# Own steps of a 7x7 depthwise convolution: eleven dealt stores, and bands and a first tile asked for by GpSimd

## The chip, the core and the metric

The kernel runs on one core of one Trainium2 chip. The metric is the device time of one execution in microseconds (us); a time is the median of several runs. Traces and pages come from one profiled execution, whose own time stands beside its span.

## The reference

The input x is (8, 96, 96, 192) in f32. Two layers follow each other; everything is f32.

```python
x1  = x  + L0(gn(x))      # gn: group norm, 32 groups
out = x1 + L1(gn(x1))

def L0(v):                # 192 -> 384 -> 192 channels
    local = conv3x3_depthwise(v @ W_in + b_in)
    mixed = 0.25 * (four directional EMA scans of local) + local
    return (layernorm(mixed) * ln_g + ln_b) @ W_out + b_out

def L1(v):                # 192 -> 768 -> 192 channels
    y = conv7x7_depthwise(v) + dw_bias
    y = gelu((layernorm(y) * ln_gamma + ln_beta) @ w0 + b0)
    return (y @ w1 + b1) * gamma
```

The group norm takes its sums over a whole image, so the 7x7 convolution of one half of the batch can begin when x1 of that half is complete.

## The kernel before

The order of the instructions on each engine is written out by hand: inside `tc.manual_schedule()` every engine gets its instructions in the order in which the program names them. A DMA is issued by an engine's queue (SyncE's is `SPq` in the trace, ScalarE's `ACTq`, GpSimd's `POOLq`), and a wait at the head of such a queue holds all that is behind it. Tiles come from pools; a tile whose place in memory was used before waits for the last user of that place.

The work runs in five stages. Times in brackets are those of the profiled execution, counted from the start of the span.

- Stage A: group norm of x and the projection W_in.
- Stage B: the 3x3 convolution, the four scans, their mixing.
- Stage C (to about 2633 us): layer norm, W_out and the residual. It makes x1 in tiles `x1c` (line 1097), 12 tiles in all, from a pool `c_x` of two buffers. Each tile is written to the DRAM array `X1` by `store_c` (line 1133) in 12 stores of 384 KB, in runs of 768 bytes. One store goes out with each unit of work (`stores.pop(0)()`); those of the last tile are left over at the end of the loop and are issued on SyncE in one go (`for store in stores: store()`).
- Stage D, the "own" steps (2630 to about 2960 us): steps n = 0 to 18 of the 7x7 convolution, with `NI` = 16 and `N1` = 19. Step n has a channel group of 12 channels and half of the batch. It needs six loads of x1 (`load_raw`, line 887, 384 KB each, tiles `raw`, three pairs numbered t), the convolution's weights written as a band matrix (`load_band`, line 897, 624 KB, tile `band`; `spread`, line 925, copies it to the other 64 partitions), the group norm applied to the raws (`scale_steps`, lines 919 and 921, tile `xin`), the matmuls (`conv_d`, line 1244, 144 a step in the trace), 12 evictions by ScalarE that add the bias (line 1254, tile `yo`), and stores of the result to the DRAM array `Y` (`store_d`, lines 1271, 1275, 1276: two of 810 KB and four of 27 KB, on SyncE). Raws are asked for two steps ahead by GpSimd, bands two steps ahead by SyncE. `yo` has two buffers, so step n's evictions wait for the stores of step n-2.
- Stage E (2960 us to the end): the last pass over 144 tiles of Y, `y_n`. `load_y` (lines 1305 and 1311, tiles `ya` and `yb`, 40 loads each: 32 of them of 60 KB, in runs of 384 bytes) fetches a tile; `norm_steps_e` gives the chain of its layer norm (sums, line 1388; `total`, 1354 to 1362; centering, 1381; square, on ScalarE; powers, 1415, on GpSimd); lines 1451 and 1461 are the matmuls with w0, 1481 those with w1, 1492 the residual, 1500 the output. The other steps of the convolution (19 to 31) are spliced into it.

The first tiles of the last pass are loaded while the own steps still run. `main_y` names 24 loads of y_0, which go out between the channels of own steps 12, 13 and 14, two after each `conv_d(n, c)`, on ScalarE's queue. `rest_y` holds the tile's memory set-up (n = 11), the other 16 loads of y_0 (n = 16, after the convolution) and the 40 loads of y_1 (n = 17), the last two on SyncE. In own step 17 the layer norm's chain for y_0 begins (`chain`), and in step 18 that for y_1 (`nxt`). The scalings of xin for step 18 are `steps[:per_t]` on VectorE (those of t = 0) and `on_scalar` on ScalarE (t = 1, 2).

The order of one own step, in the loop over n, is: raws of n + 2, band of n + 2, stores of n - 1, then the scalings for n + 1, then the convolution of n, then `on_scalar` and `rest_y`.

Of the kernel before, what the change touches and what calls it, by code (L numbers as in the profile page):

```python
# [8 lines left out]
F32 = mybir.dt.float32  # L9
# [92 lines left out]
def conv_blocks_kernel(  # L102
# [31 lines left out]
    nc = tc.nc  # L134
    B, S, _, D = x.shape
# [10 lines left out]
    by_tile = dict(reuse_waits="tile")  # L146
# [18 lines left out]
    WQ = WV // NV  # L165
# [85 lines left out]
    with ExitStack() as ph:  # L251
        cp = ph.enter_context(tc.tile_pool(name="a_const", bufs=1, **by_tile))
        xp = ph.enter_context(tc.tile_pool(name="a_x", bufs=6, **by_tile))
# [259 lines left out]
        with tc.manual_schedule():  # L513
# [71 lines left out]
    NI = len(place)  # L585
# [212 lines left out]
    NI = D // GC  # L798
# [92 lines left out]
    def load_band(n, eng=None):  # L891

        i = todo[n][1]
        pool = early if n >= N1 else (early, gp, d_pools[1])[n % 3]
        bands[n] = band = pool.tile([128, GC, ZW], F32, tag="band", name="band1")
        g = i % 2
        (eng or nc.sync).dma_start(
            band[g * 64 : (g + 1) * 64].rearrange("q c l -> q (c l)"),
            Z2_d[:, i * GC : (i + 1) * GC].rearrange("r c l -> r (c l)"),
        )  # L900
# [104 lines left out]

    with ExitStack() as ph:
        cp = ph.enter_context(tc.tile_pool(name="c_const", bufs=1, **by_tile))
        xp = ph.enter_context(tc.tile_pool(name="c_x", bufs=2, **by_tile))
        ip = ph.enter_context(tc.tile_pool(name="c_in", bufs=4, **by_tile))
        sp = ph.enter_context(tc.tile_pool(name="c_small", bufs=2, **by_tile))  # L1010
        ps_s = ph.enter_context(tc.tile_pool(name="c_ps_s", bufs=1, space=PSUM, **by_tile))
# [3 lines left out]
        NJ3 = 3  # L1015
# [9 lines left out]
                pick[:, b], ident[:, b * QH : b * QH + 1].to_broadcast([128, 128])  # L1025
            )
        nc.vector.memset(mean_w, 1.0 / C)
        lnb = xp.tile([128, NJ3, D, WQ], F32, tag="x1c", name="lnb")
        lnb = lnb.rearrange("p j c v -> p (j c v)")[:, : NC * 128]
        lnb = lnb.rearrange("p (m k) -> p m k", m=NC)  # L1030
        ps = ps_s.tile([128, 512], F32, tag="gn_ps", name="ps_w")
# [109 lines left out]
        steps, stores, first_d = [], [], []  # L1141
        with tc.manual_schedule():
            weights = load_weights()
            for u in range(n_u + 1):
                if weights and u >= 8:
                    with nc.allow_non_contiguous_dma(reason="one value per partition"):
                        nc.scalar.dma_start(*weights.pop(0))
                if u + 3 < n_u:
                    ahead.append(load_c(u + 3))
                if stores:  # L1150
                    stores.pop(0)()
                if u == n_u - 36:
                    early_d = [lambda: load_band(0)]
                    early_d += [lambda t=t: load_raw(0, t) for t in range(NT)]
                    early_d += [lambda: load_band(1)]
                if u >= n_u - 36 and u % 3 == 0 and early_d:
                    early_d.pop(0)()
                if u == n_u - 14:
                    first_d += scale_steps(0)
                    for t in range(NT):  # L1160
                        first_d.insert((t + 1) * 9 - 1, lambda t=t: load_raw(1, t))
                if u >= n_u - 14:
                    for step in first_d[:3]:
                        step()
                    del first_d[:3]
                if held is not None:
                    rs = scale_c(held[1])
                if u < n_u:
                    mt, xr = ahead.pop(0)
                    nc.gpsimd.tensor_tensor(  # L1170
                        xr, xr, cst.unsqueeze(1).to_broadcast([128, NJ3, D]), ALU.add
                    )
                    var = sp.tile([128, NJ3], F32, tag="var", name="var")
                    pa = ps_o.tile([128, 2, D + 1], F32, tag="po", name="po")
                    pb = ps_o.tile([128, 2, D + 1], F32, tag="po", name="po")
                    pos = [pa[:, 0], pa[:, 1], pb[:, 0]]
                    for j in range(NJ3):
                        block_c(mt, pos[j], var, j)
                if steps:
                    for step in steps.pop(0):  # L1180
                        step()
                if held is not None:
                    n, v = divmod(u - 1, WQ)
                    if v == 0:
                        x1c = xp.tile([128, NJ3, D, WQ], F32, tag="x1c", name="x1c")
                    finish_c(x1c, v, held[0], rs, held[2])
                    if v == WQ - 1:
                        steps += group_steps(x1c, n)
                        stores += [
                            lambda x=x1c, n=n, j=j, q=q: store_c(x, n, j, q)  # L1190
                            for j in range(NJ3)
                            for q in range(NX)
                        ]
                held = (pos, var, xr) if u < n_u else None
            for step in first_d:
                step()
            for store in stores:
                store()
            for step in sum(steps, []):
                step()  # L1200

    WE = 8
    NJ3 = 3
# [58 lines left out]
    def store_d(n):  # L1262

        hf, i = todo[n]
        yf = yos.pop(n).rearrange("q l n c v -> q l (n c v)")
        e = 3 * PH
        m = HG * PH
        for k in range(2):
            part, at = divmod(2 * i + k, YG)
            y_d = Y_d[hf][part][:, at].rearrange("r b a n -> r (b a n)")  # L1270
            nc.sync.dma_start(
                y_d[e : e + NB * m].rearrange("(l q) n -> q l n", q=m),
                yf[k * 64 + e : k * 64 + e + m],
            )
            nc.sync.dma_start(y_d[:e], yf[k * 64 : k * 64 + e, 0])
            nc.sync.dma_start(y_d[ROWS - e :], yf[k * 64 + KB - e : k * 64 + KB, NB - 1])
# [228 lines left out]
    with tc.manual_schedule():  # L1505
        with tc.tile_pool(name="d_own", bufs=1, side="right", **by_tile) as own:
            d_pools[1] = own
            make_xin(1)
            load_band(2)
            make_yo(1)  # L1510
            norms = norm_c(1, bank)
            y_0, y_1 = load_y(0), load_y(1)
            main_y = {
                NI - 4: [y_0[1 + q * 5 + b] for q in (0, 1) for b in range(NH)],
                NI - 3: [y_0[1 + q * 5 + b] for q in (2, 3) for b in range(NH)],
                NI - 2: [y_0[1 + q * 5 + b] for q in (4, 6) for b in range(NH)],
            }
            rest_y = {
                NI - 5: y_0[:1],
                NI: [y_0[1 + q * 5 + b] for q in (5, 7) for b in range(NH)]  # L1520
                + [y_0[1 + q * 5 + NH] for q in range(8)],
                NI + 1: y_1,
            }
            for n in range(N1):
                if n + 2 < N1:
                    for t in range(NT):
                        load_raw(n + 2, t)
                    if n:
                        load_band(n + 2)
                if n:  # L1530
                    store_d(n - 1)
                if n >= 3 and norms:
                    norms.pop(0)()
                if n == 10:
                    make_weights(bank())
                steps = scale_steps(n + 1) if n + 1 < N1 else []
                last, on_scalar = [], []
                if n == NI + 1:
                    chain = norm_steps_e(0)
                    per_t = len(steps) // NT  # L1540
                    on_scalar = steps[per_t:-1]
                    steps = steps[-1:] + chain[:3] + steps[:per_t]
                    on_scalar.insert(per_t, chain[3])
                    chain = chain[4:]
                elif n == NI + 2:
                    nxt = norm_steps_e(1)
                    steps = chain[:2] + nxt[:3] + chain[2:]
                    on_scalar = nxt[3:4]
                    chain = nxt[4:]
                for step in steps:  # L1550
                    step()
                for c in range(GS):
                    conv_d(n, c)
                    for step in main_y.get(n, [])[2 * c : 2 * c + 2]:
                        step(nc.scalar)
                for step in on_scalar + rest_y.get(n, []):
                    step()
            store_d(N1 - 1)
            load_band(N1)
            for t in range(NT - 1):  # L1560
                load_raw(N1, t)
# [8 lines left out]
        for n in range(N1, len(todo)):  # L1570
            more = n + 1 < len(todo)
            scales = scale_steps(n)
            per_t = len(scales) // NT
# [28 lines left out]
        for u in range(n_u + 1):  # L1602
            n, t = divmod(u, per)
# [5 lines left out]
            norm, chain = chain, norm_steps_e(u + 2) if u + 2 < n_u else [lambda: None] * 7  # L1609
# [81 lines left out]
```

## Time and profile before

| | |
|---|---|
| Median of 3 runs | 5508.98 us (5501.92 to 5525.27) |
| Profiled execution | 5497.31 us, of which the span is 5495.5 us |
| Mean granted clock of TensorE | 0.983 |
| TensorE busy | 5277.4 us, 96% of the span, 42206 matmuls |
| VectorE / ScalarE / GpSimd busy | 63% / 47% / 43% of the span |
| DMA traffic | 1015 MB, mean 185 GB/s |

In the profile's groups the own steps' convolution and stage E's convolution steps share line 1244 (4608 matmuls, 420.7 us busy, with 95.7 us idle before them). A row of the timeline reads: start in us, length in us, engine, line of the program, operation, output <- inputs, tile sizes, count, and in square brackets the idle time before it and what ended it. A `q` behind an engine's name is its DMA queue, where a row spans the first issue to the end of the last. A row of the windows gives for one stretch of time each engine's busy time and instruction count, the granted clock, the share of time that the 16 DMA engines were busy, and GB/s.

### The profile page before, as it was taken

To read this page: it belongs to the slowest core of one execution; us is meant where nothing else is said; L and a number is where in the kernel's file an instruction comes from. 1 tells how busy PE (TensorE), PEld (TensorE's weight loads), DVE (VectorE), ACT (ScalarE), POOL (GpSimd) and SP (SyncE) were. 2 spreads that over 40 slices of the span, in tenths; PEclk is the share of its full clock that TensorE was granted. 3 is DMA by queue.
4 is the path that set the end of the run, shared out by engine and by line. 5 is a ranking of instruction groups with operands and counts; after the bars stand their busy time and mean duration, and the time that the engine had idled before them with its cause. 6 is when DMAs were issued, how large, how long until landed. Compare 5 with 4: busy or idle time off the path is not lost. (4 is left out here: it accounts for less than half of the span.)

```text
span 5495.5 us, 108054 instructions
## 1 busy us (share of the span) xinstructions
PE 5277.4 (96%) x42206; PEld 3357.6 (61%) x42206; DVE 3449.8 (63%) x6722; ACT 2586.1 (47%) x5778; POOL 2367.0 (43%) x2060
## 2 busy tenths in 40 slices
PE   6999989999999899999787899999999999999999
PEld 4666643333333799899444566666666676766767
DVE  6556549999999455555555545555566666656654
ACT  2444447777777466565434444444433333333332
POOL 1211128888888555555322232222233333333332
PEclk9999989999999999999888999999999999999999
DMA  7999869999998799899997454555433232333231
GB/s 219 286 289 276 244 188 245 244 244 243 245 243 218 233 291 294 263 287 308 287 302 176 120 137 121 131 138 136 114 89 80 79 79 79 88 90 86 79 79 41
DMA packets 793246, 1015.28 MB, mean 185 GB/s; under 512 B 331151, under 2 KB 668768, under 8 KB 790688
## 3 DMA queue, kind: packets, MB, share of 16 engines
q1 hardware_dynamic: 676488, 633.41, 44.1%
q0 software_dynamic: 84848, 334.59, 18.5%
q10 hardware_dynamic: 31400, 40.37, 3.3%
q8 instruction: 333, 5.46, 0.4%
q14 instruction: 177, 1.45, 0.1%
HBM read 603.70 MB, written 419.95 MB: 186 GB/s over the span
## 5 line engine op out<-in xcount | busy, mean ns | idle before, releaser
L1481 PEld LDWEIGHTS hp<-w1g,g 128*128 128x128 f32 x6912 | 1117.9, 190 | 140.7 <-issue 83.4
L1481 PE MATMUL hp<-w1g,g 128*128 128x192 f32 x6912 | 1174.9, 329 | 0.0
L1470 ACT ACTIVATE g<-hp,b0g 128x512 f32<-128x512 f32 x864 | 519.8, 692 | 1209.4 <-PE hp L1461 1186.1
L1500 POOL DMA_DIRECT2D out_dram<-xo x288 | 211.3, 734 | 1569.5 <-DVE xo L1492 1488.0
L1492 DVE TENSOR_TENSOR xo<-hp,r 128x384 f32<-128x384 f32 x288 | 229.1, 795 | 983.5 <-PE hp L1481 979.2
L1451 PE MATMUL hp<-yT,w0w 128*128 128x512 f32 x1728 | 779.3, 597 | 19.6 <-DVE yT L1436 19.6
L1080 PE MATMUL po<-wc,mt 128*128 128x193 f32 x3456 | 685.5, 334 | 9.8 <-DVE x1c L1097 9.2
L662 PE MATMUL pl<-pin,band 34*32 34x380 f32 (+1 forms) x13824 | 629.4, 490 | 17.5 <-issue 17.5
L746 POOL TENSOR_TENSOR mo<-mo,z 128x768 f32<-128x768 f32 x286 | 598.9, 2094 | 4.5 <-ACT mo L687 0.4
L1080 PEld LDWEIGHTS po<-wc,mt 128*128 128x128 f32 x3456 | 554.9, 191 | 41.3 <-ACT mean L1082 30.8
L1451 PEld LDWEIGHTS hp<-yT,w0w 128*128 128x128 f32 x1728 | 321.3, 190 | 379.7 <-issue 346.0
L695 DVE TENSOR_TENSOR_SCAN z<-decay,loc 128x768 f32<-128x768 f32 x288 | 505.9, 1757 | 38.7 <-ACT loc L671 9.6
L1244 PE MATMUL hp<-xin,band 63*64 63x372 f32 (+1 forms) x4608 | 420.7, 501 | 95.7 <-ACT yo L1254 35.2
L704 DVE TENSOR_TENSOR_SCAN z<-decay,z 128x768 f32<-128x768 f32 x288 | 498.4, 1731 | 0.1
L662 PEld LDWEIGHTS pl<-pin,band 34*32 34x32 f32 x13824 | 236.1, 107 | 392.8 <-issue 385.9
L1415 POOL TENSOR_TENSOR rs<-tot,neg_half 32x32 f32<-32x32 f32 x72 | 394.7, 5481 | 120.3 <-DVE tot L1413 92.5
L683 PE MATMUL pa<-loc,mix 128*32 128x384 f32 x3456 | 431.9, 493 | 0.0
L686 PE MATMUL pa<-last,down 96*32 96x384 f32 x1152 | 426.8, 493 | 0.9 <-ACT mo L687 0.9
L1461 PE MATMUL hp<-yT,w0w 64*128 64x512 f32 x1728 | 419.5, 611 | 0.0
L1254 ACT ACTIVATE yo<-hp,dwb 128x384 f32<-128x384 f32 x384 | 197.0, 584 | 435.6 <-PE hp L1244 285.0
L671 ACT COPY loc<-pl 128x384 f32<-128x384 f32 x576 | 248.0, 483 | 310.7 <-PE pl L662 310.7
L395 PE MATMUL pm<-xT,win 128*128 128x384 f32 x1152 | 392.4, 491 | 0.0
(155 smaller groups left out, 7237.6 us busy)
## 6 DMA issues: line engine op xcount, KB each, us to landing
pin<-P SPq DMA_DIRECT2D x192, 576.0 KB
P<-po POOLq DMA_DIRECT2D x95, 1152.0 KB, 9.9
mt<-M SPq DMA_DIRECT2D x192, 384.0 KB
xq<-in_x_dram SPq DMA_DIRECT2D x96, 576.0 KB
xr<-in_x_dram SPq DMA_DIRECT2D x192, 288.0 KB
X<-x1c SPq DMA_DIRECT2D x144, 384.0 KB
out_dram<-xo POOLq DMA_DIRECT2D x288, 192.0 KB, 2.5
r<-X SPq DMA_DIRECT2D x35, 1536.0 KB
```

The lines of the kernel that those rows point to most:

```text
L662: nc.tensor.matmul(pls[g][at * RB : (at + 1) * RB, :, lo:hi], band[rows, c, kh, :], pin[rows, c, :, NJ - 1 - j, lo + kh - 1 : hi + kh - 1] ...
L683: nc.tensor.matmul(pa[at], mix[:, i, at], loc[:, q], start=True, stop=True)
L686: nc.tensor.matmul(pa[at], down[:, to], last[:, q], start=True, stop=True)
L695: nc.vector.tensor_tensor_scan(zf, decay_f, loc.rearrange("p q n -> p (q n)"), 0.0, ALU.mult, ALU.add)
L704: nc.vector.tensor_tensor_scan(zr, decay_f, zr, 0.0, ALU.mult, ALU.add)
L746: eng.tensor_tensor(m, m, z, ALU.add)
L1080: nc.tensor.matmul(po, lhs[m], wc[:, m], start=(m == 0), stop=(m == NC - 1))
L1244: nc.tensor.matmul(pys[g][k * 64 : (k + 1) * 64, :, lo:hi], band[rows, k * GS + c, d * ZS : d * ZS + 64], xin[rows, :, :, k * GS + c, lo + ...
L1451: nc.tensor.matmul(hps[m, q], w0w[:, 0, m * 128 : (m + 1) * 128], yT[:, 2 * q], start=True, stop=False,)
L1461: nc.tensor.matmul(hps[m, q], w0w[p, 1, m * 128 : (m + 1) * 128], yT[p, 1], start=False, stop=True,)
L1470: nc.scalar.activation(g[:, m, q], hps[m, q], AF.Gelu, bias=b0g[:, m : m + 1], scale=1.0)
L1481: nc.tensor.matmul(po[:, q], g[:, m, q, k * 128 : (k + 1) * 128], w1g[:, m], start=(m == 0), stop=(m == NE - 1),)
```

## The change

Five things change; the arithmetic does not.

1. The pool `c_x` of two buffers becomes two pools of one buffer each, `xps[0]` and `xps[1]`, taken in turn, the last tile x1c from `xps[0]`. So each of the two has its own place in memory, and the pool of the own steps, `d_own`, lies over the other one.
2. The 12 last stores of x1 are not issued at the end of stage C. They are kept in `late_x` and issued on SyncE in the own steps: two in step 0, one each in steps 1 to 10, after the stores of step n - 1.
3. Bands 2 to 18 are issued by GpSimd instead of SyncE (bands 0, 1 and 19 stay).
4. y_0's loads go to GpSimd: the 24 of `main_y` come from ScalarE's queue, the 16 of `rest_y` at n = 16 from SyncE's. Those of y_1 stay on SyncE.
5. In step 17 the eight scalings of t = 0 stand ahead of the first three steps of the layer norm's chain on VectorE, instead of behind them.

```diff
-        xp = ph.enter_context(tc.tile_pool(name="c_x", bufs=2, **by_tile))
+        xps = [
+            ph.enter_context(tc.tile_pool(name=f"c_x{n}", bufs=1, **by_tile)) for n in range(2)
+        ]
...
-                        x1c = xp.tile([128, NJ3, D, WQ], F32, tag="x1c", name="x1c")
+                        x1c = xps[1 - n % 2].tile([128, NJ3, D, WQ], F32, tag="x1c", name="x1c")
...
             for step in first_d:
                 step()
-            for store in stores:
-                store()
+            late_x = stores
             for step in sum(steps, []):
                 step()
...
-            load_band(2)
+            load_band(2, nc.gpsimd)
...
                     if n:
-                        load_band(n + 2)
+                        load_band(n + 2, nc.gpsimd)
                 if n:
                     store_d(n - 1)
+                for step in late_x[: 1 if n else 2]:
+                    step()
+                del late_x[: 1 if n else 2]
...
-                    steps = steps[-1:] + chain[:3] + steps[:per_t]
+                    steps = steps[-1:] + steps[:per_t] + chain[:3]
...
                 for c in range(GS):
                     conv_d(n, c)
                     for step in main_y.get(n, [])[2 * c : 2 * c + 2]:
-                        step(nc.scalar)
-                for step in on_scalar + rest_y.get(n, []):
+                        step(nc.gpsimd)
+                for step in on_scalar:
                     step()
+                for step in rest_y.get(n, []):
+                    if n == NI:
+                        step(nc.gpsimd)
+                    else:
+                        step()
```

More of the change, by code (lines that the diff above doesn't have):

```diff
@@ L1027, in conv_blocks_kernel @@
         nc.vector.memset(mean_w, 1.0 / C)
-        lnb = xp.tile([128, NJ3, D, WQ], F32, tag="x1c", name="lnb")
+        lnb = xps[0].tile([128, NJ3, D, WQ], F32, tag="x1c", name="lnb")
         lnb = lnb.rearrange("p j c v -> p (j c v)")[:, : NC * 128]
```

## The prediction

> **What bounds the kernel now.** I read the page's slices first. A slice is 137.4 us (5495.5 / 40).
>
> ```profile
> PE   6999989999999899999787899999999999999999
> ...
> DMA  7999869999998799899997454555433232333231
> ```
>
> TensorE is full nearly everywhere, save slice 0 and slices 19 to 22 (2610 to 3160 us). There DMA is full at first (9s in slices 19 and 20) and then falls. Every edit lies between 2610 and 2990 us. Second, the chain of work that ended last:
>
> ```profile
> PE 26%; issue 1%; DVE 0%; POOL 0%; ACT 0%; POOLq 0%
> ```
>
> From about 3072 us to the end it is TensorE alone, so a microsecond won before 3072 us arrives whole at the end, and so does one lost. Third, the windows of the stretch (columns: window, us, then busy us of PE, PEld, DVE, ACT, POOL, then granted clock, DMA share, GB/s):
>
> ```profile
> 2632.00:2657.00 25.00, 24.02 (x286) 11.59 (x286) 19.75 (x59) 19.82 (x43) 10.62 (x18) 0.93 1.01 254
> 2657.00:2680.00 23.00, 0.75 (x7) 0.29 (x2) 0.29 (x1) 1.05 (x2) 0.00 (x0) 0.56 1.07 293
> 2680.00:2840.00 160.00, 142.24 (x1572) 81.87 (x1570) 105.23 (x295) 59.94 (x120) 54.19 (x68) 0.93 1.02 319
> 2840.00:2908.00 68.00, 51.68 (x493) 33.88 (x497) 26.89 (x77) 24.09 (x48) 13.35 (x19) 0.84 0.97 254
> ```
>
> The 16 DMA engines are full (share 0.97 to 1.07) for 276 us, while TensorE idles 23 + 16 us in two of the windows. An own step moves 6 raws of 384 KB, a band of 624 KB and stores of 2 x (810 + 27 + 27) KB: 4656 KB, 4.77 MB, 14.9 us at 319 GB/s. Its 144 matmuls take 12.3 us (142.24 / 1572 x 144 = 13.0 with gaps). **So transfers pace these steps, and a wait taken from TensorE there is a gain only if the same bytes then move at a higher rate.** Last, the timeline: whom TensorE waits for, and what the queues did then.
>
> ```profile
> 2679.62 1.51 PE L1244 MATMUL hp<-xin,band 63*64 63x384 f32 x2 [22.25 <-DMA band<-Z_d]
> 2841.09 7.63 PE L1244 MATMUL hp<-xin,band 63*64 63x384 f32 x72 [6.66 <-ACT yo L1254]
> 2871.12 6.08 PE L1244 MATMUL hp<-xin,band 63*64 63x384 f32 x48 [5.13 <-ACT yo L1254]
> 2944.77 14.35 PE L1244 MATMUL hp<-xin,band 63*64 63x384 f32 x144 [12.53 <-DVE T L1354]
> 2994.22 2.05 PE L1451 MATMUL hp<-yT,w0w 128*128 128x512 f32 x2 [18.44 <-DVE yT L1436]
> 3072.47 3.96 PE L1244 MATMUL hp<-xin,band 63*64 63x384 f32 x24 [18.79 <-DVE band L925]
> ```
>
> ```profile
> 2619.87 51.49 SPq L1133 DMA_DIRECT2D X<-x1c  x13
> 2671.40 1.66 SPq L897 DMA_DIRECT2D band<-Z_d  x2
> ```
>
> SyncE's queue issues 13 stores of X1 one behind another, for 51 us; bands 2 and 3 come after them, and TensorE waits 22.25 us for band 2.
>
> **A: bands off SP, stores dealt, y_0's first 24 loads off ACT (own steps 0 to 15).** Removed: the 22.25 us. Added back: 12 stores of 384 KB, 4.7 MB, are no longer moved before step 2 but two in step 0 and one in each of steps 1 to 10; at 319 GB/s each adds 1.2 us to a step that is already paced by bytes, 12 x 1.2 = 14.8 us. So the removed wait by itself is worth only what is moved faster. The 48 us from 2632 to 2680 moved 25 x 254 + 23 x 293 = 13.1 MB; at 319 GB/s that is 41.1 us: 6.9 us can be won (0 if the X1 stores are slow wherever they lie). I take 6: the window at 319 GB/s holds seven X1 stores too. In the 68 us from 2840 ScalarE's queue carries the loads of y_0 among the evictions that TensorE waits for:
>
> ```profile
> 2850.56 4.11 ACTq L1305 DMA_DIRECT2D ya<-Y  x2
> 2854.72 2.00 ACT L1254 ACTIVATE yo<-hp,dwb 128x384 f32<-128x384 f32 x4 [3.60 <-issue]
> 2870.49 0.58 ACT L1254 ACTIVATE yo<-hp,dwb 128x384 f32<-128x384 f32 x1 [7.07 <-DMA ya<-Y]
> ```
>
> An eviction waits 3.6 us for two issues, another 7.07 us for a load's signal. At 319 GB/s the 68 us would be 54.1, so 13.9 us to win. Kept out of that: the y_0 loads are short runs wherever they are issued (ScalarE's queue moved 1.48 MB in 2.0% of 2600 to 2960 us, 7.2 us against 4.6 at 319 GB/s: 2.6 more than its bytes), and on GpSimd they stand in order with the raws and bands, whose issue waits for the transfer eight before it. That queue then has 6 + 1 + 8 issues in each of steps 12 to 14; at about 10 us from issue to landing (a raw takes 13.4 us in the median at full load) 15 issues in eights take 19 us against 15, up to 4 us a step, but only for the part of the raws that is not early by two steps. I take 9 (from -1, if all 3 x 4 us and the 2.6 come on, to 11). A is 15, from -1 to 18. GpSimd's extra issues, 17 bands and 40 loads at 0.62 us (a raw's 3.73 us for six), are 35 us; the POOL column above is 13 busy in 68 us, so there is room. Band 2 heads that queue and waits for x1c's place to come free, whose last store is issued at 2619.87 and landed by about 2625; TensorE first wants band 2 at 2657, so that costs nothing.
>
> **B: the rest of y_0 (16 loads) on GpSimd instead of SP, ahead of own step 18.** Before, they sit behind the stores of step 15 and hold SP for 10.2 us:
>
> ```profile
> 2922.53 6.04 SPq L1305 DMA_DIRECT2D yb<-Y  x8
> 2928.67 1.80 SPq L1311 DMA_DIRECT2D ya<-Y  x4
> 2930.52 1.85 SPq L1311 DMA_DIRECT2D yb<-Y  x4
> ```
>
> y_0 is whole at 2932.2, 24.7 us after the end of conv 15 at 2907.5, and DVE then makes its sums, and only after them xin for step 18: that is the 12.53 us wait. Band 18's issue (2911.77) no longer stands among the stores of step 15, and the 16 issues run beside SP's: I estimate y_0 whole at +18.5, 6 us won of 12.53 (0, if the queue on GpSimd holds them as long, to 10). The eight scalings of xin put ahead of the chain (2.4 us of DVE) cost nothing there, and gain nothing by themselves, since step 18 still needs ScalarE's xin behind a square of the same chain.
>
> **C: y_1 on SP starts earlier.** The 10.2 us of issues are gone ahead of the stores of step 16 and of y_1. Before, y_1's last groups meet six raws and r, 3.9 MB asked for by GpSimd within 5 us:
>
> ```profile
> 2953.41 2.20 SPq L1305 DMA_DIRECT2D yb<-Y  x4
> 2972.58 0.30 SPq L1311 DMA_DIRECT2D yb<-Y  x1
> 2976.84 1.87 SPq L1305 DMA_DIRECT2D yb<-Y  x4
> ```
>
> ```profile
> 2951.16 3.73 POOL L887 DMA_DIRECT2D raw<-X  x6
> ```
>
> One group takes 19.2 us beside them, the following ones 3.9 each. Ten microseconds sooner, two or three of the four lie ahead of the burst (10.2 / 3.9 = 2.6). The burst depends on step 18's start, which B brings 6 us nearer, so about one group's lead is lost again. The 18.44 us wait at 2994, and 1.15 behind it, should fall to 6: 13 won (0 if a group still meets the burst, 18 if none does).
>
> **D.** The 18.79 us before 3072 stand on a later tile, y_2, and a band load of ScalarE's queue, neither of them touched: 0.
>
> **Sum**: 15 + 6 + 13 = 34 us of the profiled execution's 5497.3: 5463. The median of the three runs is 5509.0, 11.7 above that execution; less 34 it is 5475.
>
> **A rule against the change.** The trace first: raws landed about every 1.83 us while X1 stores issued beside them were 8 us apart (a store's row: `2637.45 8.04 SPq L1133`), and alone they moved at 341 to 371 GB/s. The Trainium skill, "DMA: Bandwidth & Descriptors", section "Issuing engines are not separate DMA queues", has it that issuing from several engines saves only the sequencer's time, since all of it runs on the same 16 engines. By that, moving bands would save SP only about 17 x 0.45 us of issues, some 8 us in all, and the sum would end near 5500. The same page's "Queues, rings and completion order" says that each engine takes turns between queues packet by packet; that would make 768-byte stores lose against raws as in the 8 us row, and a queue of their own would then shield the bands.
>
> **The rivals.** *Slower: a dealt store holds the stores behind it.* On SP each X1 store now stands ahead of the next Y store. Beside raws it took 8.0 us in the row above. If ten steps pay that each, 81 us come against 22 (band 2's wait) and 19 (B and C): 40 slower, 5549. It decides from (22 + 19) / 10 = 4.1 us a step on. For it: yo's evictions already wait 114.4 us for Y stores. Against it: eight may be in flight, and the window at 319 GB/s includes seven such stores. 0.18. *Bytes alone:* nothing of A is kept, since the same bytes move at the same rate; B and C leave 19, 5490. 0.10. *y_1 meets the burst all the same:* A and B, 21 won, 5488. 0.10. *All of both stretches:* A 22, B 10, C 18: 50 won, 5459. 0.13. *It doesn't do what it says:* band 2 waits on GpSimd as long as it did on SP, and y_0 as well: 5509. 0.04. The forecast itself has 0.45.
>
> **How the numbers follow.** A difference below 0.5%, 27.5 us, is about what a measurement of this kernel cannot tell from none. Faster than 5481.4: the forecast and "all of both", 0.58. Within: 0.24. Slower: 0.18. The range reaches from 5448 (50 won, and 11.7 of the runs' own spread) to 5530, which takes in the cases at 5488, 5490 and 5509 and stops short of the slower one; the forecast's own range is 5459 to 5490.
>
> **What would show it.** Right: the 22.25 us wait for band 2 gone, steps 0 to 10 about 1.2 us longer each, no ACT wait on issues or `ya` between 2840 and 2908, the wait on `DVE T L1354` near 6, the one on `DVE yT L1436` near 6, the 18.79 unchanged. Wrong: evictions' waits for Y stores well above 114 us in steps 1 to 11 (the slower rival); raws late behind `ya` on GpSimd; a `yb` group still of 19 us.

## The result and the profile after

The changed kernel takes 5501.14 us in the median of 20 runs, the kernel before 5506.38: a ratio of 0.9991, 95% interval 0.9982 to 1.0. That is at most 0.2%, where 0.6% (34 us) was forecast. The profiled execution takes 5497.68 us with a span of 5495.9 (before 5497.31 and 5495.5). Line numbers of the changed kernel are one to three higher: the convolution's matmuls are L1245, the evictions L1255, Y's stores L1272 to L1277, X1's L1135. The dealt stores are twelve, in eleven steps.

The page's slices look as before. The windows of the stretch, with the same columns and the same cuts as in the prediction, and one more behind them:

```profile
2632.00:2657.00 25.00, 22.99 (x272) 11.37 (x276) 21.50 (x60) 20.11 (x44) 11.32 (x19) 0.93 0.97 240
2657.00:2680.00 23.00, 18.15 (x207) 11.19 (x200) 11.89 (x36) 7.84 (x16) 7.06 (x11) 0.93 1.03 305
2680.00:2840.00 160.00, 122.81 (x1362) 70.66 (x1355) 87.35 (x250) 54.72 (x108) 48.79 (x66) 0.87 0.99 300
2840.00:2908.00 68.00, 52.36 (x590) 32.28 (x586) 30.16 (x85) 26.64 (x52) 29.10 (x46) 0.90 0.99 291
2908.00:2960.00 52.00, 24.20 (x248) 14.60 (x244) 27.55 (x70) 20.29 (x38) 18.75 (x25) 0.72 0.74 185
```

TensorE now works in the second window (18 us instead of 0.75). The third pays for it: 122.8 us busy instead of 142.2, and the DMA engines, nearly as full as before (0.99), move 300 GB/s instead of 319. The fourth has gained (590 matmuls instead of 493), the fifth is where it goes again (248 instead of 428). The fifth before the change:

```profile
2908.00:2960.00 52.00, 38.14 (x428) 28.93 (x421) 36.34 (x89) 28.31 (x56) 10.30 (x8) 0.87 0.69 179
```

TensorE's larger waits in the changed kernel, by the timeline:

```profile
2694.62 6.29 PE L1245 MATMUL hp<-xin,band 63*64 63x384 f32 x48 [9.87 <-ACT yo L1255]
2800.71 6.16 PE L1245 MATMUL hp<-xin,band 63*64 63x384 f32 x48 [12.26 <-ACT yo L1255]
2899.76 14.21 PE L1245 MATMUL hp<-xin,band 63*64 63x384 f32 x144 [7.57 <-DMA band<-Z_d]
2955.52 14.81 PE L1245 MATMUL hp<-xin,band 63*64 63x384 f32 x144 [18.56 <-ACT xin L919]
2998.04 5.06 PE L1452 MATMUL hp<-yT,w0w 128*128 128x512 f32 x6 [6.67 <-DVE yT L1437]
3073.30 4.04 PE L1245 MATMUL hp<-xin,band 63*64 63x384 f32 x24 [18.59 <-DVE band L925]
```

The 22.25 us for band 2 are gone. In their place stand waits for evictions, the longest in steps 3, 6 and 9 (9.87, 9.40 and 12.26 us; the evictions themselves wait for Y's stores there), waits for bands in steps 15 to 17 (6.06, 7.57 and 9.24), and a longer one before step 18. The two before the second tile's matmuls are 3.31 and 6.67 us, before 18.44 and 1.15, and the last one is as it was.

To compare kernels I use marks: the end of an own step's last eviction (rows of L1254, L1255), counted from the end of step 0, and TensorE's resumption for step 19 (3072.47 before). Counting from step 0 matters, since the profiled executions reach it anywhere from 2645 to 2676 us, for reasons that lie before every edit here (two kernels that leave out stores also change stage C). From the resumption to the end all kernels take 2420 to 2425 us. Six kernels that are alike up to step 11 have that mark at 177.9 to 182.7, and three others at 154.0 to 160.0: differences below 5 or 6 us say little.

| us from the end of step 0 | step 11 | step 15 | step 17 | step 18 | resumption |
|---|---|---|---|---|---|
| before | 180.9 | 261.5 | 286.2 | 313.1 | 425.4 |
| changed | 188.0 | 245.0 | 289.7 | 323.1 | 425.0 |

By stretches: steps 1 to 11 lose 7.1, steps 12 to 15 win 23.6 (80.6 to 57.0), steps 16 and 17 lose 20.0 (24.7 to 44.7), step 18 loses 6.5 (26.9 to 33.4), and from there to the resumption 10.4 are won (112.3 to 101.9). The sum is 0.4 us. The change does a great deal, and nearly all of it cancels.

### The profile page after: what moved, and what is told of

It reads as the page before. It is cut to its first block, busy times and chain, and to the rows that moved or that the text cites. A ratio compares the mean times of both kernels' runs of the same rounds, so it can differ in the third digit from the quotient of the medians.

```text
span 5495.9 us, 108079 instructions
## 1 busy us (share of the span) xinstructions
PE 5274.1 (96%) x42206; PEld 3344.9 (61%) x42206; DVE 3453.3 (63%) x6722; ACT 2592.7 (47%) x5778; POOL 2397.4 (44%) x2117
## 5 line engine op out<-in xcount | busy, mean ns | idle before, releaser
L1245 PE MATMUL hp<-xin,band 63*64 63x372 f32 (+1 forms) x4608 | 416.3, 502 | 110.9 <-ACT yo L1255 44.0
L1255 ACT ACTIVATE yo<-hp,dwb 128x384 f32<-128x384 f32 x384 | 198.5, 583 | 437.6 <-PE hp L1245 306.8
```

The lines of the kernel that those rows point to most:

```text
L1245: nc.tensor.matmul(pys[g][k * 64 : (k + 1) * 64, :, lo:hi], band[rows, k * GS + c, d * ZS : d * ZS + 64], xin[rows, :, :, k * GS + c, lo + ...
```

## Experiments: one part of the change at a time

Two theories stood at the start. "Bytes": the stage is paced by transfers, so the dealt stores repay what the wait gave. "Queue": the loss is made in GpSimd's queue, where bands and y_0 stand with the raws.

**Dealt stores alone** (bands, y_0, order as before). Against the changed kernel:

```diff
-            load_band(2, nc.gpsimd)
+            load_band(2)
...
-                        load_band(n + 2, nc.gpsimd)
+                        load_band(n + 2)
...
-                    steps = steps[-1:] + steps[:per_t] + chain[:3]
+                    steps = steps[-1:] + chain[:3] + steps[:per_t]
...
-                        step(nc.gpsimd)
+                        step(nc.scalar)
...
-                    if n == NI:
-                        step(nc.gpsimd)
-                    else:
-                        step()
+                    step()
```

> Only the two pools and the dealt stores of x1; bands on SyncE and y_0 asked for as before. Marks in the trace (last eviction of an own step, us): before 2828.0 for step 11, 2908.6 for step 15, 2933.3 for step 17, 2960.2 for step 18; changed kernel 2836.3, 2893.3, 2938.0, 2971.4. Theory 'bytes' (the stage is paced by transfers, and X1 stores beside raws, bands and Y stores lower the rate): the 22 us wait for band 2 is gone, but step 11 ends at about 2836 all the same, and the time is that of before or up to 8 us more (5506 to 5514). Theory 'queue' (the loss sits in GpSimd's own queue, where bands and y_0 stand with the raws): step 11 ends by 2820, and the time is 10 to 20 us less (5486 to 5496).

Measured: 5507.39 us, ratio 1.0012 (0.9994 to 1.003). Marks: step 11 at 189.3, step 17 at 295.1, resumption 431.0. As "bytes" had it, the stores by themselves make steps 1 to 11 longer, by 8 us.

**Bands alone** on GpSimd. Against the kernel before:

```diff
-            load_band(2)
+            load_band(2, nc.gpsimd)
...
-                        load_band(n + 2)
+                        load_band(n + 2, nc.gpsimd)
```

> Only the bands 2 to 18 on GpSimd; the 12 stores of x1 stay in a burst on SyncE, y_0 as before. Theory 'bytes': band 2 is there at once, but the Y stores of steps 0 and 1 stand behind the burst, so that step 2 or 3 waits for yo instead; step 11 ends within 3 us of 2828, time within 5 us of before. Theory 'queue': each band holds raws on GpSimd for its turn of the signals, so step 11 ends 5 to 15 us later than 2828, and the time rises by as much.

Measured: 5505.73 us, ratio 1.0002 (0.9989 to 1.0016). Band 2 is there, and step 2 waits 38.4 us for evictions instead, since the Y stores of steps 0 and 1 stand behind the burst. Step 11 is at 188.7 (8 us later, the mark that "queue" gave), the resumption at 428.2; the time stays, as "bytes" had it. The 22 us wait was never a gain to be had by itself: the next thing behind the burst waits in its place.

**Both, without y_0's move.** The diff of the dealt stores alone, without its first two changes:

```diff
-                    steps = steps[-1:] + steps[:per_t] + chain[:3]
+                    steps = steps[-1:] + chain[:3] + steps[:per_t]
...
-                        step(nc.gpsimd)
+                        step(nc.scalar)
...
-                    if n == NI:
-                        step(nc.gpsimd)
-                    else:
-                        step()
+                    step()
```

> Dealt stores and bands on GpSimd; y_0's loads and the order in step 17 as before. Theory 'bytes': step 11 as in the changed kernel (2836), then steps 12 to 17 as slow as before (105 us), so step 17 ends at about 2941 and the time is some 5 us above before. Theory 'queue': step 11 at 2836, and steps 12 to 17 faster than in the changed kernel (under 102 us).

Measured: 5510.0 us, ratio 1.0014 (1.0 to 1.0028); step 11 at 189.1, step 17 at 297.4, resumption 428.8. Steps 12 to 17 take 108.3 us, not under 102: "queue" fails here, and so far bands and stores together do no more than either.

**y_0 alone** on GpSimd (stores in a burst, bands on SyncE). Against the kernel before:

```diff
-                        step(nc.scalar)
-                for step in on_scalar + rest_y.get(n, []):
+                        step(nc.gpsimd)
+                for step in on_scalar:
                     step()
+                for step in rest_y.get(n, []):
+                    if n == NI:
+                        step(nc.gpsimd)
+                    else:
+                        step()
```

> Only y_0's 40 loads on GpSimd; stores in a burst, bands on SyncE, order in step 17 as before. Both theories: up to step 11 as before (2828.0). Theory 'bytes': what steps 12 to 14 win (34 us in the changed kernel: 71 us before, 37 after) is lost again in steps 15 to 17 (34 before, 65 after), because raws 15 to 18 and bands come late, so step 17 ends within 4 us of 2933; y_1 then comes sooner, time 0 to 10 us less. The prediction's step B would have step 18 begin 6 us sooner and the time 20 us less.

Measured: 5480.82 us, ratio 0.9964 (0.9945 to 0.9982), resumption 401.7: 24 us sooner. Steps 12 to 15 take 60.5 us (80.6 before), and steps 16 and 17 give back 6.7 of it, not all. "Bytes" is wrong here, and the changed kernel holds a gain that its other parts take back.

**The last 16 loads of y_0 alone** (the first 24 stay on ScalarE). Against y_0 alone:

```diff
-                        step(nc.gpsimd)
+                        step(nc.scalar)
                 for step in on_scalar:
```

> Of y_0's loads only the last 16 on GpSimd, the first 24 on ScalarE as before; stores in a burst, bands on SyncE, the old order. The prediction's steps B and C by themselves: step 15 as before (261.5), step 18 six us sooner (307), resumption 19 sooner (406). If the first 24 loads are what wins, step 18 at 313 and the resumption at 416 to 425.

Measured: 5495.03 us, ratio 0.999 (0.9973 to 1.0006), resumption 417.2, step 18 at 313.0. Before step 18 the wait is 13.71 us (12.53 before): step B of the prediction brings nothing, step C brings 8. The other 15.5 us of y_0's move (417.2 less 401.7) come from taking the first 24 loads off ScalarE's queue.

**The changed kernel with bands back on SyncE.**

```diff
-            load_band(2, nc.gpsimd)
+            load_band(2)
...
-                        load_band(n + 2, nc.gpsimd)
+                        load_band(n + 2)
```

> The changed kernel with bands 2 to 18 back on SyncE: dealt stores, y_0 on GpSimd, the new order in step 17. Marks counted from the end of own step 0 (end of step 11, 15, 17, 18, and TensorE's resumption for step 19): before 180.9, 261.5, 286.2, 313.1, 425.4; changed kernel 188.0, 245.0, 289.7, 323.1, 425.0; y_0 alone 177.9, 238.4, 269.7, 296.9, 401.7. Theory 'one queue too full': bands and y_0 together on GpSimd are what makes steps 15 to 17 late, so without the bands step 11 is at 188, step 15 at 248, step 17 at 279, the resumption at 411: 14 us less than before. Theory 'dealt stores': the bands do nothing, step 17 is at 290 and the resumption at 425.

Measured: 5495.62 us, ratio 0.9986 (0.9972 to 1.0); step 11 at 186.2, step 17 at 283.1, step 18 at 307.6, resumption 412.3, 13 us sooner than with the bands on GpSimd. "One queue too full" forecast 411.

**The changed kernel with a burst again** (bands and y_0 on GpSimd).

```diff
-            late_x = stores
+            late_x = []
+            for store in stores:
+                store()
```

> The changed kernel with the 12 stores of x1 in a burst again: bands and y_0 on GpSimd, the new order in step 17. Theory 'one queue too full': step 11 at about 188 (as with bands alone on GpSimd), step 17 at 290, resumption at 425, time as before. Theory 'dealt stores': step 17 at 278 and resumption at 410.

Measured: 5498.14 us, ratio 0.9991 (0.9977 to 1.0005); step 17 at 283.3, resumption 417.6. Neither forecast is met (425 and 410).

**The order in step 17**, on top of y_0 alone.

```diff
-                    steps = steps[-1:] + chain[:3] + steps[:per_t]
+                    steps = steps[-1:] + steps[:per_t] + chain[:3]
```

> y_0 on GpSimd and the new order in step 17, the rest as before. The prediction puts the eight moved scalings at nothing, since step 18 waits for ScalarE's scalings behind the chain's square: step 18 and the resumption as in y_0 alone (296.9, 401.7), within 3 us. Rival: the scalings ahead of the chain delay the sums by 2.4 us, and step 18 with them (299 and 404).

Measured: 5480.46 us (5480.82 without it), ratio 0.9964 (0.9949 to 0.9979), resumption 404.4. The resumption is 2.7 us later than in y_0 alone, which the marks don't tell from nothing; the time is the same, and from step 11 to step 18 both take as long (119.4 and 119.0 us). So the order is worth nothing that shows, as the prediction had it. Against this kernel the parts now add up: dealt stores +7.9 (412.3), bands +13.2 (417.6), both +20.6 (425.0). Without y_0 on GpSimd they were +5.6, +2.8 and +3.4. So the bands cost ten microseconds more where y_0's loads share their queue.

**What y_0's loads do in that queue, and what the bands add.** GpSimd's waits at the head of its queue between 2840 and 2960 us in the changed kernel:

```profile
POOL yb L1306 <- DMA raw<-X: 17.7, 12, 2.8
POOL ya L1306 <- DMA raw<-X: 17.2, 12, 3.7
```

The columns are the total, the times and the longest. 24 times a load of y_0 waits for an earlier raw, 35 us in all, and what follows waits with it. But with the bands back on SyncE those waits are as long (the same stretch from step 0, 2837 to 2957):

```profile
POOL ya L1306 <- DMA raw<-X: 17.9, 10, 3.8
POOL yb L1306 <- DMA raw<-X: 17.1, 13, 3.1
```

So they are not the bands' price. What they hold up in both kernels is raws. VectorE's scalings wait for raws in these stretches, for 29.7 us in the changed kernel and 35.4 with the bands on SyncE; in the kernel before they wait for no raw between 2840 and 2960. Of the two, only the changed kernel has a wait for bands beside it:

```profile
DVE xin L921 <- DMA raw<-X: 29.7, 9, 10.0
DVE band L925 <- DMA band<-Z_d: 14.4, 4, 13.3
```

With the bands on SyncE the first row is:

```profile
DVE xin L921 <- DMA raw<-X: 35.4, 9, 10.3
```

Behind y_0's loads, bands 17 and 18 are issued at 2904.91 and 2919.31, 256.6 and 271.0 us after step 0; on SyncE they went out at 224.9 and 240.5. Band 17 lands at 273.3, and the matmuls of step 17 begin at 274.9 instead of 268.5. y_0's last loads go out by 2942.30, 294.0 us after step 0 instead of 280.4, and the wait before step 18 is 18.56 us instead of 11.32. (Before the change, y_0's last loads on SyncE were out by 2932.)

**Price of the stores.** Two kernels issue no store of x1's last tile in the own steps.

```diff
+                        if n == 2 * n_s - 2:
+                            stores += [
+                                lambda x=x1c, n=n, j=j, q=q: store_c(x, n + 1, j, q)
+                                for j in range(NJ3)
+                                for q in range(NX)
+                            ]
...
-            for store in stores:
-                store()
```

That is the kernel before; in the changed one the last lines are `late_x = stores`, which becomes `late_x = []`. In stage C two stores a unit go out over the last tile.

> The kernel before, with no store of x1's last tile in the own steps: its place in X1 gets the tile before it, stored in stage C (the values of that sixth of one half are not x1's). It prices the 12 stores in a burst. Marks from the end of own step 0. Theory 'bytes': 4.7 MB at 312 GB/s, so step 11 at 181 - 15 = 166. If the burst costs by its wait of 22 us as well: 159. The time falls by as much as step 18's mark does.

> The same with the changed kernel: no dealt stores of x1's last tile (the same values are not x1's), bands and y_0 on GpSimd. If dealt stores cost more than their bytes, step 11 is at 166 as in the kernel of before without them, so their price is 22 us against 15 in a burst. If the loss lies with the bands on GpSimd, step 11 stays 5 to 8 us later than in the kernel of before without them (171 to 174).

Measured: without the burst 5492.22 us, step 11 at 164.8: its price is 16.1 us (180.9 less 164.8), as its bytes say (15). (The resumption is 19 us sooner, the time 12 us shorter; stage C differs too.) The changed kernel without its dealt stores takes 5468.45 us, ratio 0.9938 (0.9915 to 0.9961), step 11 at 155.0: the price of the same stores, dealt, is 33.0 us (188.0 less 155.0), twice their bytes. With the bands on SyncE the same price is 24.5 us (189.3 less 164.8). Against the forecast the bands on GpSimd made steps 1 to 11 shorter, not longer, once the stores are gone.

## Experiments: whose queue the stores stand in

SyncE's waits between 2640 and 2840 us in the changed kernel:

```profile
SPq L1276 <- DMA Y<-yo: 51.4, 12, 6.6
SPq L1272 <- ACT yo L1255: 48.7, 9, 14.2
SPq L1272 <- DMA X<-x1c: 43.0, 6, 9.4
```

Six Y stores wait 43.0 us at the head of the queue until an X1 store has landed, and the evictions of the step after next wait for those Y stores. That is the "slower" rival of the prediction. The trace tells which X1 store: the DMAs of SyncE and ScalarE take one of eight signals in turn (GpSimd's have another eight), and each waits until the DMA that had its signal before has landed. SyncE issues seven DMAs a step here, so the Y store behind an X1 store has the signal of the X1 store of the step before. With the bands on SyncE there are eight a step: an X1 store then always has the signal of the X1 store before it, and it is the X1 stores that wait for one another (36.2 us in steps 1 to 11 of the dealt stores alone), with the Y stores behind them in the queue.

**Dealt stores on GpSimd** (bands on SyncE, y_0 as before). Against the dealt stores alone:

```diff
-            nc.sync.dma_start(
+            eng.dma_start(
                 X1_d[hf][r : r + 127 * NJ3 * PH + 1 : NJ3 * PH, k, a],
...
-                    step()
+                    step(nc.gpsimd)
```

> Dealt stores, but issued by GpSimd; bands on SyncE, y_0 and the order in step 17 as before. Against the same with the dealt stores on SyncE (step 11 at 189.3, every third step waiting 9 to 11 us for a Y store). Theory 'held in SyncE's queue': Y stores no longer stand behind an X1 store's signal, so step 11 comes back to about 181 and the every-third-step waits go. Theory 'rate': the stores take what they take beside raws, step 11 at 186 to 190.

Measured: 5493.41 us, ratio 0.9981 (0.9966 to 0.9997); step 11 at 171.6, against 189.3 on SyncE and 180.9 in a burst. More than "held in SyncE's queue" forecast.

**Dealt stores on ScalarE**, whose DMAs share SyncE's eight signals. Against the dealt stores alone:

```diff
-                    step()
+                    step(nc.scalar)
```

> Dealt stores issued by ScalarE; bands on SyncE, y_0 and the order in step 17 as before. Marks from the end of own step 0; dealt on SyncE step 11 is at 189.3, dealt on GpSimd at 171.6, in a burst at 180.9. Theory 'turn of signals' (a later Y store waits until an X1 store eight issues before it has landed; ScalarE and SyncE share the eight): step 11 stays at 185 to 195, and SyncE's waits for X1's landing stay. Theory 'SyncE's own queue' (the stores hold only what is in the same queue): step 11 at 170 to 176.

Measured: 5497.87 us, ratio 0.9994 (0.9978 to 1.0009), step 11 at 175.7, and SyncE waits for no X1 store any more (ScalarE does once, 12.6 us). With eight DMAs a step the X1 stores keep one signal among themselves, there as on SyncE, but here it is ScalarE's queue that waits for it; so most of the loss comes from that wait standing in SyncE's queue. Whether a shared signal alone would cost anything isn't shown, since in neither of the two a Y store gets an X1 store's signal.

**The changed kernel, its dealt stores on GpSimd** (`store_c` takes its queue as above).

```diff
                 for step in late_x[: 1 if n else 2]:
-                    step()
+                    step(nc.gpsimd)
```

> The changed kernel, its dealt stores issued by GpSimd instead of SyncE; bands and y_0 stay on GpSimd. Changed kernel: step 11 at 188.0, step 18 at 323.1, resumption at 425.0. If SyncE's queue is what the dealt stores hold up, step 11 is at 172 to 178, and the resumption 10 to 16 us sooner (409 to 415), time about 5488. If the bands on GpSimd then stand behind the stores there, step 11 stays at 185 to 190 and the time at 5501.

Measured: 5475.9 us, ratio 0.9951 (0.9933 to 0.9968); step 11 at 154.1, step 18 at 290.5, resumption 389.4. The same stores now cost nothing that shows: left out, step 11 was at 155.0. SyncE carries Y's stores alone, and most of its waiting from 2640 to 2840 us is for evictions, that is, for something to store (the first list below). The two windows behind that list are 160 us long and begin 3 us ahead of the end of step 0, the first of this kernel, the second of the changed one:

```profile
SPq L1272 <- ACT yo L1255: 133.8, 13, 26.7
SPq L1277 <- DMA Y<-yo: 24.9, 11, 5.4
```

```profile
2660.00:2820.00 160.00, 147.98 (x1692) 91.06 (x1688) 103.61 (x296) 69.19 (x138) 67.33 (x88) 0.95 1.02 354
```

```profile
2645.00:2805.00 160.00, 117.96 (x1319) 69.27 (x1311) 85.18 (x243) 54.91 (x110) 49.79 (x66) 0.87 1.01 302
```

354 GB/s at a DMA share of 1.02, where the changed kernel has 302 at 1.01, and TensorE busy for 148.0 us instead of 118.0. Both theories of the start fall for steps 1 to 11: it is not the bytes, and it is not GpSimd's queue. That the stores are free belongs to this kernel, in which TensorE is nearly full; without them it is busy for as long (148.3 of 160 us). With the bands on SyncE the same stores on GpSimd cost 6.8 us (171.6 less 164.8).

One more thing differs between the two engines. X1's stores are records of 768 bytes on SyncE and ScalarE, and none of GpSimd's DMA records has that size; the DMA packets of the two windows, of the changed kernel and of this one, are:

```profile
DMA packets 17386, 48.39 MB, mean 302 GB/s; under 512 B 1825, under 2 KB 7012, under 8 KB 16796
DMA packets 16500, 56.56 MB, mean 354 GB/s; under 512 B 2104, under 2 KB 3355, under 8 KB 15835
```

That could be a cause of its own. ScalarE speaks against it as the main one: with records of 768 bytes step 11 came 13.6 us sooner there than on SyncE, of the 17.7 that GpSimd brought. In windows of 160 us from 3 us ahead of the end of step 0, those three kernels move 295 GB/s (SyncE), 321 (ScalarE) and 330 (GpSimd), all at a share of 1.01 or 1.02. With the bands on GpSimd, where the gain is largest, the two causes were not taken apart.

## Experiments: versions that beat both

**The square last.** On ScalarE, the square of y_0's chain comes behind all scalings for step 18 (with y_0 on GpSimd, stores in a burst, bands on SyncE).

```diff
-                    on_scalar.insert(per_t, chain[3])
+                    on_scalar.append(chain[3])
```

> y_0 on GpSimd, the old order on VectorE, but ScalarE's square of the chain in step 17 comes after all its scalings for step 18 instead of between those of t = 1 and t = 2. If the square is what holds step 18: VectorE's scalings still stand behind the chain's mean and centering there, so little, at most 5 us of the 13.4 us wait; the resumption at 397 to 402. If the chain as a whole is what counts, nothing: 402.

Measured: 5476.53 us, ratio 0.995 (0.9934 to 0.9967), resumption 398.0 (401.7 without). The wait before step 18 is 7.7 us instead of 13.4. Its own share of the time is within the noise.

**Raws of step 20 on GpSimd**, on top of that.

```diff
-                    slots[t - 3].append(lambda n=n, t=t: load_raw(n + 1, t, nc.scalar))
+                    slots[t - 3].append(
+                        lambda n=n, t=t: load_raw(n + 1, t, nc.gpsimd if n == N1 else nc.scalar)
+                    )
```

> y_0 on GpSimd, the square last in step 17, and in the last pass the raws of step 20 asked for by GpSimd instead of ScalarE. The wait of 20 us before step 19's matmuls is put down to SyncE's loads of y_2 standing behind ScalarE's issue of these raws in the shared turn of signals. If so, the wait falls below 8 us and the time is 12 to 20 us under the 5476 of the kernel without this edit. If y_2's loads wait for a free tile or for bytes instead, the wait stays at 18 to 20 us and the time with it.

Measured: 5461.0 us, ratio 0.9913 (0.9894 to 0.9931), resumption 379.4. The wait that the change left as it was, 20.15 us without this edit, is gone:

```profile
3024.36 2.12 PE L1244 MATMUL hp<-xin,band 63*64 63x384 f32 x24 [0.85 <-DVE band L925]
```

**Everything that won, together.** Against the changed kernel, beside the two diffs above and the bands back on SyncE:

```diff
                 for step in late_x[: 1 if n else 2]:
-                    step()
+                    step(nc.gpsimd)
...
-                    steps = steps[-1:] + steps[:per_t] + chain[:3]
+                    steps = steps[-1:] + chain[:3] + steps[:per_t]
```

> Everything that won, together: dealt stores on GpSimd, bands on SyncE, y_0 on GpSimd, the square last in step 17, raws of step 20 asked for by GpSimd. Without the dealt stores on GpSimd it was 5461.0, resumption at 379.4. If the gains add (9 us from the dealt stores on GpSimd), the resumption is at about 371 and the time at 5452; if GpSimd's queue is too full with stores, raws and y_0, 5461 or more.

Measured: 5446.18 us, ratio 0.9903 (0.988 to 0.9926), step 11 at 171.3, resumption 371.4: by the marks the gains add (371 was forecast); by the times the interval overlaps that of the kernel without the dealt stores on GpSimd (0.9894 to 0.9931).

**The same, with bands 2 to 12, or all of them, on GpSimd.** The split; for all of them the condition goes:

```diff
-            load_band(2)
+            load_band(2, nc.gpsimd)
...
-                        load_band(n + 2)
+                        load_band(n + 2, nc.gpsimd if n < 11 else nc.sync)
```

> Dealt stores on GpSimd, bands 2 to 12 on GpSimd and 13 to 18 on SyncE, y_0 on GpSimd, the old order in step 17 with the square last, raws of step 20 on GpSimd. Marks from the end of own step 0. Theory 'bands and y_0 in one queue make steps 15 to 18 late': step 11 at 154, then as with all bands on SyncE (60 to step 15, 119 to step 18): step 18 at 273, resumption at 354, time near 5430. Rival 'the lead is lost anyway, since steps 12 to 18 are held by y_0's loads': step 18 at 285 to 291, resumption at 366 to 372, time near 5446.

> The same with bands 2 to 18 all on GpSimd. Theory 'bands and y_0 in one queue': step 11 at 154, step 18 at 285 to 291, resumption at 366 to 372, time 5440 to 5446, so 12 to 18 us more than with bands 13 to 18 on SyncE. Rival: no difference between the two.

Measured: split 5449.75 us, ratio 0.9895 (0.9876 to 0.9915), step 11 at 154.0, step 18 at 285.6, resumption 370.5. All on GpSimd 5445.4 us, ratio 0.9892 (0.9873 to 0.9912), step 11 at 160.0, step 18 at 299.1, resumption 379.3. The intervals of the three overlap: the times don't tell them apart. Of the split's lead of 17 us at step 11, 5 are left by step 18, as the rival said, with bands 13 to 18 on SyncE too. What holds steps 12 to 18 in these kernels is not settled. All three beat both kernels by about 1%.

## Why the prediction was wrong

Two steps of its sum failed. In A it took a full DMA share for a bound by bytes and put the dealt stores at their bytes alone, and in A and B it held GpSimd's queue to have room for bands and y_0. Gains as large came in steps 12 to 15 and behind step 18; that the time came out level, inside the stated range, is luck. In the order of the sum, in us won:

| term | forecast | measured in the change | by itself |
|---|---|---|---|
| A, steps 1 to 11 | +6 | -7.1 | -8.4 (stores), -7.8 (bands) |
| A, steps 12 to 15 | +9 | +23.6 | +15.5 (24 loads off ScalarE, on the resumption) |
| A, GpSimd's queue, steps 16 and 17 | 0, up to 4 a step | -20.0 | -6.7 (y_0 alone) |
| B | +6 | -6.5 | 0 (last 16 loads) |
| C | +13 | +10.4 | +8 (last 16 loads) |
| D | 0 | 0 | 0 |

**A, the dealt stores.** The prediction took 319 GB/s at a share of 1.0 for what the DMA engines can move, and so let the wait of 22 us turn into bytes and 6 us of rate. It took the 6 because "the window at 319 GB/s holds seven X1 stores too". In the kernel before it holds none: all of them are issued by 2671.4, and the issues from 2680 to 2840 us are

```profile
raw<-X POOLq DMA_DIRECT2D x66, 384.0 KB, 13.5
Y<-yo SPq DMA_DIRECT2D x21, 810.0 KB
band<-Z_d SPq DMA_DIRECT2D x11, 624.0 KB
Y<-yo SPq DMA_DIRECT2D x41, 27.0 KB
```

With X1 stores among them in SyncE's queue the changed kernel moves 300 there, and they cost 33.0 us instead of the sum's 14.8: steps 1 to 11 lose 7.1 where 6 were to be won. The runs show a share of 1.0 at 302 and at 354 GB/s in these steps; what changed between the two is the queue that issues the X1 stores, and with it the size of their records. The "slower" rival had the mechanism right, a dealt store holding the Y store behind it in SyncE's queue, with 43.0 us of such waits. Its price was too high: 33.0 us over ten steps is 3.3 each, not 8.0, and below the 4.1 from which that rival was to decide. Its sign did not come either: between 2632 and 2960 us evictions wait 98.6 us for Y stores, less than the 114.4 before.

**A, the loads off ScalarE.** The mechanism held, and the bound of 11 us, again from 319 GB/s, was too low. No eviction waits for a load of `ya` any more, and steps 12 to 15 take 57.0 us.

**A, GpSimd's queue.** The step that failed most, with its conclusion "the POOL column above is 13 busy in 68 us, so there is room": busy time says nothing of a queue that waits. The text counted 15 issues in a turn of eight, up to 4 us a step. Its range allowed 12 us for that, its value took 2, since raws are two steps early. In place of that, y_0's loads wait 35 us for raws, the raws behind them come late, and the loss falls into steps 16 and 17, which take 20.0 us more. How much of that comes with y_0's loads alone the marks leave open: with the bands on SyncE these two steps take 6.7 (y_0 alone) to 16.9 us more (the changed kernel with bands back on SyncE). Bands in that queue cost 10 us more, on the resumption, with y_0 there than without.

**B.** y_0 is not whole sooner: the last loads are issued on GpSimd at 2940, behind all of that, and the wait before step 18 is 18.56 us, where 6 was forecast. The rival "band 2 waits as long, and y_0 as well" had its second half right. Even without bands and the other 24 loads in the queue (last 16 loads alone) B is nothing: that wait is 13.71 us.

**C and D** were right, C by 10.4 for 13. y_1's loads are out by 2960.84 and the six raws follow at 2961.48, so that no group meets them. Part of that is luck: the burst came 9 us later, counted from step 0, where B was to bring it 6 us nearer. With the last 16 loads alone C is 8. D stayed; the prediction put it on y_2 and a band load, and the wait went when the raws of step 20 left ScalarE's queue. The scalings put ahead of the chain are worth nothing that shows, as written. The Trainium skill, "DMA: Bandwidth & Descriptors", section "Issuing engines are not separate DMA queues", would leave the issuing engine only the sequencer's time. These runs disagree: with the bands on GpSimd the same twelve stores cost 33.0 us on SyncE and nothing measurable on GpSimd (155.0 without them, 154.1 with).

## What to carry to other kernels

A wait that ends on one queue tells what stands behind it as well: before taking it away, list what is next in that queue, and give the stores that free a double buffer a queue with nothing slow in it. Do not turn a full DMA share into a bound by bytes; try the same bytes from another engine's queue first. Where a change has parts, time each by itself, since one that wins 24 us was here hidden under two that lost nearly as much.

## What the runs showed of the hardware

- A DMA share of about 1.0 went with 302 and with 354 GB/s over 160 us of own steps. The program differs only in the engine that issues one store a step; the sizes of that store's DMA records differ with it.
- Dealt stores of 384 KB in runs of 768 bytes cost 33.0 us in SyncE's queue among Y's stores with the bands on GpSimd, and 24.5 with the bands on SyncE. In GpSimd's queue they cost nothing that the marks can tell, and 6.8. On ScalarE, in another queue but on SyncE's eight signals, step 11 came 13.6 us sooner than on SyncE (175.7 against 189.3). Why one queue's transfers slow the whole set was not tried further.
- Loads of 60 KB dealt among loads of 384 KB in GpSimd's queue wait for the large ones at its head: 35 us for y_0's, with the bands in that queue or not.
